# The delta rule's triangular inverse: the level of 16 made by a second substitution on VectorE, the first one moved a turn earlier, and the lanes reordered

## The chip, the core and the metric

The kernel runs on one core of a Trainium2 chip. The core has five engines that run at the same time, each through its own queue of instructions in order: TensorE (matrix products; PE in the profile, its weight loads PEld), VectorE (DVE), ScalarE (ACT), GpSimd (POOL) and SyncE (SP), which here issues every DMA. The metric is device time in microseconds (us): the median of a few runs. The profile is one further execution, and has a time of its own.

## The reference

A network of two layers works on 1024 tokens of width 256. Each layer is half an FFN, attention, and half an FFN. The first layer's attention is a windowed softmax attention; the second layer's is a gated delta rule, and only that one is touched here. It has 16 heads with keys and values of 128 channels:

```python
def step(S, inp):
    qt, kt, vt, gt, bt = inp
    S = S * gt[..., None]
    pred = jnp.einsum('bhk,bhkv->bhv', kt, S)
    delta = (vt - pred) * bt[..., None]
    S = S + kt[..., None] * delta[:, :, None, :]
    o = jnp.einsum('bhk,bhkv->bhv', qt, S)
    return (S, o)
```

The kernel does not walk through 1024 steps. It takes chunks of 128 tokens. In a chunk the steps are a triangular system: with M the gated products of the chunk's keys below the diagonal and beta the step sizes, the kernel needs Z, the inverse of a triangular 128x128 matrix, once for each chunk and head. All arithmetic is float32.

## The kernel before

The first 600 us are the first layer and an FFN, the last 60 an FFN; the delta rule (`delta_rule`, from L509) lies between. Its 16 heads are four groups of four (HG); a group has eight chunks, taken two at a time. So there are 16 **pairs** (one group, two chunks: eight triangular matrices), and the work of a pair is made of generators that yield after each step:

- `prepare` (L664): convolves keys and queries (`convolved`, L633: two products on TensorE, one scaling on ScalarE, three multiply-adds on VectorE for each head), norms, gates. It stores `cfd`, the 1024 numbers of beta, to DRAM for `solve` (L687).
- `triangle` (L773): for the levels 1, 2, 4, ..., 64 it multiplies keys with gated keys and queries (`pm`, L791), and gates them further on VectorE (L813) and GpSimd (L819). A level n gives the blocks of M that join two neighbours of size n. Levels below 16 are gathered in the tile `ml` (L854), level 16 in `mt16` (L856), 32 in `mt32`, 64 in `mt64`. After the loop's level 32 it stores `ml` to DRAM as `dm` (L843).
- `solve` (L879): loads the 16x16 diagonal blocks of `dm` back, one block to a partition (`xb`, 64 partitions, L888), and `cfd` as `diag`; inverts all 64 blocks by substitution on VectorE (L899 to L937); stores the inverted blocks and their transposes to DRAM as the block diagonals of two zeroed matrices (L949), and loads those as `z` and `zt` (L951, L954).
- `invert` (L957): doubles the inverted blocks, from 16 to 32, from 32 to 64 and from 64 to 128, on TensorE: `pmz` = M Z (L968), a negating copy `mz` on ScalarE (L976), `dz` (L983, L991), and a copy into `z` and `zt`. For level 16 that copy is three predicated copies on VectorE (L1008, L1010).
- `values` (L745), `gates` (L756): the values' convolution and the output gate.
- `advance` and `emit` (L1038, L1081): the recurrence from chunk to chunk with `zt`, and the output of a chunk.

In turn i (L1130) the lanes work on different pairs: `prepare` on pair i+2, `triangle` on i+1, `solve`, `invert`, `values`, `gates` on i, `advance` and `emit` on i-1. `weave` (L1111) emits their steps by a list written by hand: a lane has a begin, an end (as fractions of the turn) and a count of steps, and its steps are spread evenly between. That sets the order of the program. It is not yet the order on the engines: the kernel is built with `schedule_with_timeline_sim=True` (L1257), where a planner may move an instruction ahead of others on its engine when its own estimate of times says that it is ready.

Most tiles that the change touches have one buffer (the pool `blk`, bufs=1), `ml`, `mt32` and the two DRAM matrices have two, taken in turn (`turns`, L600).

Of the kernel before, what the change touches and what calls it, by code (L numbers as in the profile page):

```python
# [10 lines left out]
F32 = mybir.dt.float32  # L11
# [497 lines left out]
def delta_rule(tc, a, x, xnT, pp, bc, kon, ones, kdw, first):  # L509
# [33 lines left out]
    with ExitStack() as ctx:  # L543
# [57 lines left out]
        for i in range(2):  # L601
            turn = {}
            for nm in ("ml", "mt16", "mt32"):
                turn[nm] = cst.tile([P, 2, HG, 64], F32, name=f"{nm}_{i}")
                nc.gpsimd.memset(turn[nm], 0.0)
            for nm in ("z", "zt"):
                turn[nm] = dram.tile([2, HG, P, P], F32, name=f"{nm}_{i}", bufs=1)
                for c in range(2):
                    for r in range(2):
                        nc.sync.dma_start(  # L610
                            out=turn[nm][c].rearrange("h r s -> r h s")[:, :, 64 * r : 64 * r + 64],
                            in_=turn["mt16"][:, c],
                        )
# [159 lines left out]
        def triangle(us):  # L773
# [11 lines left out]
            for i, n in enumerate(LEVELS):  # L785
# [43 lines left out]
                if n == 32:  # L829
# [8 lines left out]
                    for c, u in enumerate(us):  # L838

                        dm = u["dm"] = dram.tile([HG, P + 1, 64], F32, name="dm", bufs=4)  # L840
                        for half in (lo, hi):
                            r0 = half.start + half.start // 64
                            nc.sync.dma_start(  # L843
                                out=dm[:, r0 : r0 + 64, :].rearrange("h r s -> r h s"), in_=turn["ml"][half, c]
# [8 lines left out]
                if n < BLK:  # L853
                    nc.vector.copy_predicated(dst(flat(turn["ml"])), pred4, run4(pm[:, 0]))  # L854
                else:
                    nc.vector.tensor_mul(dst(flat(turn["mt16"])), run4(pm[:, 0]), run4(all_heads(mask)))  # L856
# [15 lines left out]
        def blocks(ap):  # L872
# [3 lines left out]
                tensor=ap.tensor, offset=ap.offset, ap=[[BLK * (pitch + 1), P // BLK], [pitch, BLK], [1, BLK]]  # L876
            )

        def solve(us, vb):  # L879
# [5 lines left out]
            for c, u in enumerate(us):  # L885
                for h in range(HG):
                    q0 = 32 * c + 8 * h
                    nc.sync.dma_start(  # L888
                        out=xb[q0 : q0 + 8].rearrange("b (i j) -> b i j", j=BLK),
                        in_=blocks(u["dm"][h]),  # L890
                    )
# [49 lines left out]
            )  # L941
            z = us[0]["z2"] = lev.tile([P, 2, HG, 64], F32, name="z", bufs=1)
            zt = us[0]["zt2"] = lev.tile([P, 2, HG, P], F32, name="zt", bufs=2)
            for c, u in enumerate(us):
                for got, to in ((zb, "z"), (ztb, "zt")):
                    full = u["p"]["turn"][to][c]
                    for h in range(HG):
                        q0 = 32 * c + 8 * h
# [312 lines left out]
```

## Time and profile before

| | |
|---|---|
| median of 3 runs | 1785.18 us (1783.14 to 1787.38) |
| the profiled execution | 1795.66 us, of which the span of the core's instructions 1793.8 us |
| delta rule, about | 605 to 1730 us |
| mean granted TensorE clock | 0.897 |
| DMA, q1, share of 16 engines | 12.8% |

The profile's page and the trace give instructions in groups: line of the kernel, engine, operation, the tiles written and read (out<-in), their shapes and count, then the busy time in us and the mean of one in ns, and after the second bar how long the engine stood idle before them and what ended that. A view of waits says who waited for whom, in total us, times and the longest. "SPq" is a DMA being issued on SyncE's queue; if its duration is long, SyncE waited inside that row. The duration in such a row is not the transfer. The page's chain of waits goes back from the last instruction to what released it; its largest shares by line are 5% for the products of the convolutions (L641) and 4% for DMA `dm<-ml`.

### The profile page before, as it was taken

The page shows a single profiled execution, that of the slowest core. Times are in us where ns is not written, and L with a number is a line of the kernel's source. Part 1 is how long each engine was busy: PE and PEld are TensorE (multiplying, and loading weights), DVE is VectorE, ACT ScalarE, POOL GpSimd, SP SyncE. Part 2 cuts the span into 40 slices and gives each one's busy share as a digit, 9 for nine tenths or more (in the row PEclk, how much of TensorE's full clock was granted, in tenths as well). Part 3 has the DMA queues.
Part 4 walks back from the last instruction along what each step waited for, and adds up shares of the span by engine and source line. Part 5 has one row for each costly group of instructions (what it writes and reads, how often), then busy time and mean ns, then how long its engine had stood idle before and what let it go on. Part 6 is the DMA issues. An engine that isn't in the chain of part 4 may idle for free.

```text
span 1793.8 us, 33380 instructions
## 1 busy us (share of the span) xinstructions
PE 1532.6 (85%) x13152; PEld 1107.1 (62%) x13152; DVE 1186.9 (66%) x2569; ACT 831.3 (46%) x1981; POOL 526.4 (29%) x470
## 2 busy tenths in 40 slices
PE   7886868777999766789989889898999898998879
PEld 3434445545555555667767677677778776776745
DVE  3999977584232357667678678876768877877221
ACT  2117273746122344536645645654665564563320
POOL 0022223231001034335434434433434442543100
PEclk9997989889999766789889989989889988989989
DMA  7020000002002001021111121102120120111100
GB/s 241 32 54 26 3 19 1 1 1 66 0 0 47 1 7 23 10 52 28 24 15 43 21 56 22 30 12 44 38 50 15 22 47 9 40 24 23 56 0 24
DMA packets 150348, 54.94 MB, mean 31 GB/s; under 512 B 116784, under 2 KB 142704, under 8 KB 149936
## 3 DMA queue, kind: packets, MB, share of 16 engines
q1 hardware_dynamic: 150192, 52.81, 12.8%
q8 instruction: 104, 1.70, 0.4%
q14 instruction: 52, 0.43, 0.1%
HBM read 39.11 MB, written 11.70 MB: 28 GB/s over the span
## 4 chain that ended last, share of the span: by engine, by line
PE 41%; DVE 26%; ACT 11%; DMA 9%; issue 6%; POOL 4%; SPq 3%; another core or an unknown queue 1%; DVEq 0%; POOLq 0%; ACTq 0%
PE ps L641 5%; DMA dm<-ml 4%; PE po L160 4%; PE pg L135 3%; PE pu L135 3%; DVE kq L813 3%; ACT e L319 3%; PE pm L791 2%; PE pr L253 2%; DVE k L655 2%; PE pg L700 2%; PE px L1101 2%; DVE other L195 2%; PE po L365 2%; DVE other L208 2%
## 5 line engine op out<-in xcount | busy, mean ns | idle before, releaser
L819 POOL TENSOR_TENSOR k<-k,d 128x512 f32<-128x512 f32 x96 | 149.7, 1559 | 312.2 <-PE pm L791 190.6
L791 PE MATMUL pm<-kq,k 128*64 128x64 f32 x3072 | 133.5, 235 | 29.9 <-POOL kq L742 11.5
L791 PEld LDWEIGHTS pm<-kq,k 128*64 128x64 f32 x3072 | 113.3, 146 | 62.0 <-issue 40.0
L813 DVE TENSOR_TENSOR kq<-kq,d 128x1024 f32<-128x1024 f32 x96 | 130.8, 1363 | 17.8 <-PE pm L791 6.7
L319 ACT ACTIVATE e<-ps,nm 128x128 f32<-128x128 f32 x256 | 91.5, 397 | 63.6 <-DVE nm L314 62.3
L655 DVE SCALAR_TENSOR_TENSOR k<-ps,pp,k 128x256 f32<-128x256 f32 x192 | 84.7, 473 | 27.0 <-ACT k L653 25.5
L655 DVE SCALAR_TENSOR_TENSOR q<-ps,pp,q 128x256 f32<-128x256 f32 x192 | 86.2, 478 | 22.7 <-ACT q L653 20.0
L655 DVE SCALAR_TENSOR_TENSOR v<-ps,pp,v 128x256 f32<-128x256 f32 x192 | 87.5, 474 | 19.8 <-ACT v L653 18.5
L253 PE MATMUL pr<-xnT,wq 128*128 128x512 f32 x128 | 64.7, 641 | 22.1 <-DVE nm L314 10.6
L641 PE MATMUL ps<-xnT,wv 128*128 128x259 f32 x256 | 79.5, 439 | 2.7 <-DVE v L655 1.5
L983 PE MATMUL dz<-mz,zt 64*64 64x32 f32 x768 | 74.9, 230 | 8.0 <-ACT mz L976 8.0
L991 PE MATMUL dz<-zt,mz 64*64 64x32 f32 x1024 | 81.4, 234 | 0.0
L641 PE MATMUL ps<-xnT,wq 128*128 128x259 f32 x256 | 78.6, 442 | 0.4 <-DVE ss L681 0.2
L365 PE MATMUL po<-wo,oT 128*128 128x256 f32 x256 | 64.1, 394 | 13.7 <-ACT oT L362 12.4
L991 PEld LDWEIGHTS dz<-zt,mz 64*64 64x64 f32 x1024 | 67.3, 147 | 12.4 <-issue 10.6
L1101 PE MATMUL px<-wdo,oT 128*128 128x256 f32 x256 | 70.4, 421 | 5.1 <-ACT oT L1097 5.1
L641 PE MATMUL ps<-xnT,wk 128*128 128x259 f32 x256 | 71.8, 418 | 1.0 <-ACT k L653 0.5
L742 POOL TENSOR_TENSOR kq<-q,ge 128x1024 f32<-128x1024 f32 x16 | 51.3, 3209 | 70.3 <-PE pso L1073 40.0
L653 ACT ACTIVATE q<-ps,pp 128x256 f32<-128x256 f32 x64 | 30.4, 474 | 89.1 <-PE ps L641 86.5
L968 PE MATMUL pmz<-z,mt 64*64 64x64 f32 x1024 | 56.1, 233 | 18.0 <-DMA z<-z 13.7
L968 PEld LDWEIGHTS pmz<-z,mt 64*64 64x64 f32 x1024 | 42.9, 140 | 44.4 <-issue 17.8
L708 ACT ACTIVATE gy<-pg,pp 128x256 f32<-128x256 f32 x64 | 29.4, 474 | 85.4 <-PE pg L700 67.5
(215 smaller groups left out, 3953.5 us busy)
## 6 DMA issues: line engine op xcount, KB each, us to landing
zt<-zt SPq DMA_DIRECT2D x32, 256.0 KB
dm<-ml SPq DMA_DIRECT2D x64, 64.0 KB
z<-z SPq DMA_DIRECT2D x64, 64.0 KB
wq<-in_aWq SPq DMA_DIRECT2D x1, 2048.0 KB
wo<-in_aWo SPq DMA_DIRECT2D x1, 2048.0 KB
wk<-in_dWk SPq DMA_DIRECT2D x4, 512.0 KB
wq<-in_dWq SPq DMA_DIRECT2D x4, 512.0 KB
wv<-in_dWv SPq DMA_DIRECT2D x4, 512.0 KB
```

Of the source, the lines that this page charges most:

```text
L135: nc.tensor.matmul(ps[:n], lhsT=w[:, c, cs], rhs=xnT[:, c, cols], start=(c == 0), stop=(c == KC - 1))
L253: nc.tensor.matmul(pr, lhsT=w[:, c, hcol : hcol + HD], rhs=xnT[:, c, PAD + hf * 512 : PAD + (hf + 1) * 512], start=(c == 0), stop=(c == KC ...
L319: nc.scalar.activation(e[:, s, j, :], ps[:, s, j, :], AF.Exp, bias=nm[:, 4 * s + j : 4 * s + j + 1], scale=SUB**-0.5, accum_out=z[:, s, j ...
L365: nc.tensor.matmul(po, lhsT=oT[:, h, :], rhs=wpool["wo"][:, g * HG + h, :], start=(h == 0), stop=(h == HG - 1),)
L641: nc.tensor.matmul(ps[:, 0 : 2 * P + 3], lhsT=w[nm][:, c, h * HD : (h + 1) * HD], rhs=xnT[:, c, PAD + t0 - 3 : PAD + t0 + 2 * P], start=(c ...
L655: nc.vector.scalar_tensor_tensor(yh, xi, pp[:, col : col + 1], yh, ALU.mult, ALU.add)
L791: nc.tensor.matmul(pm[half, :, c * HG + h, :].rearrange("p b (s l) -> p b s l", l=n), lhsT=k[:, c, h, half], rhs=rights(kq[:, :, c, h, half]),
L813: nc.vector.tensor_mul(kqr, kqr, dl.unsqueeze(1).unsqueeze(3).to_broadcast([P, 2, 2 * HG * runs, n]),)
L819: nc.gpsimd.tensor_mul(kl, kl, dr.unsqueeze(2).to_broadcast([P, 2 * HG * runs, n]))
L968: nc.tensor.matmul(pmz[half, c, h], lhsT=p["turn"][f"mt{n}"][half, c, h], rhs=z[half, c, h], start=True, stop=True,)
L991: nc.tensor.matmul(runs(dz[half, 1, c, h]), lhsT=mz[half, c, h], rhs=right(zt[half, c, h, half], n), start=True, stop=True,)
L1101: nc.tensor.matmul(px, lhsT=oT[:, h, :], rhs=u["w"]["o"][:, h, :], start=(h == 0), stop=(h == HG - 1))
```

## The change

Level 16 is no longer made by `invert` on TensorE. `triangle` puts the products of level 16 into `ml` with the smaller ones, and `dm` then holds, beside the 16x16 blocks of the diagonal, the 16x16 blocks that join two of them. `solve` loads these too, four times over, into 128 partitions (`mb`: partition 32 j + b holds joint b, for the columns 4 j to 4 j + 3), and copies its own inverted blocks between partitions (`z1`, `z2`). A new generator, `join`, makes - Z22 M21 Z11 on VectorE by two broadcast products and two reductions, and stores the result to DRAM beside the block diagonals; then it loads `z` and `zt`, which `solve` did before. `invert` begins at 32. `solve` works on pair i+1 in the turn of its `triangle`, and not on pair i. Stores and loads of single heads are merged (`xb` one instruction, the block diagonals two). The fractions of the lanes are changed.

```diff
-                if n < BLK:
-                    nc.vector.copy_predicated(dst(flat(turn["ml"])), pred4, run4(pm[:, 0]))
-                else:
-                    nc.vector.tensor_mul(dst(flat(turn["mt16"])), run4(pm[:, 0]), run4(all_heads(mask)))
+                nc.vector.copy_predicated(dst(flat(turn["ml"])), pred4, run4(pm[:, 0]))
...
-            for c, u in enumerate(us):
-                for h in range(HG):
-                    q0 = 32 * c + 8 * h
-                    nc.sync.dma_start(
-                        out=xb[q0 : q0 + 8].rearrange("b (i j) -> b i j", j=BLK),
-                        in_=blocks(u["dm"][h]),
-                    )
+            dm = us[0]["dm"]
+            nc.sync.dma_start(
+                out=xb.rearrange("b (i j) -> b i j", j=BLK),
+                in_=blocks(dm, (BLK, BLK, 64), (1, 0, BLK), (0, 1, BLK)),
+            )
+            mb = blk.tile([P, BLK, BLK], F32, name="mb")
+            for j in range(4):
+                nc.sync.dma_start(
+                    out=mb[32 * j : 32 * j + 32],
+                    in_=blocks(dm, (32, 32, 32), (1, 0, BLK), (0, 1, BLK), col=BLK),
+                )
...
+            z1 = blk.tile([P, 4, BLK], F32, name="z1")
+            z2 = blk.tile([P, BLK, BLK], F32, name="z22")
+            for j in range(4):
+                at = slice(32 * j, 32 * j + 32)
+                nc.sync.dma_start(out=z1[at], in_=ztb[0:64:2, 4 * j : 4 * j + 4, :])
+                nc.sync.dma_start(out=z2[at], in_=zb[1:64:2])
+            rows = ((BLK, BLK, 64), (1, 0, BLK), (0, 1, BLK))
+            for got, to in ((zb, "z"), (ztb, "zt")):
+                nc.sync.dma_start(out=blocks(us[0]["p"]["turn"][to], *rows), in_=got)
+            us[0]["blocks"] = mb, z1, z2
+            yield
+
+        def join(us):
+            mb, z1, z2 = us[0]["blocks"]
+            turn = us[0]["p"]["turn"]
+            four = blk.tile([P, 4, BLK, BLK], F32, name="four")
+            nc.vector.tensor_mul(
+                four,
+                mb.rearrange("p r s -> p s r").unsqueeze(1).to_broadcast([P, 4, BLK, BLK]),
+                z1.unsqueeze(2).to_broadcast([P, 4, BLK, BLK]),
+            )
+            yield
+            mz1 = blk.tile([P, 4, BLK], F32, name="mz1")
+            nc.vector.tensor_reduce(mz1, four, AX.X, ALU.add)
+            yield
+            nc.vector.tensor_mul(
+                four,
+                z2.unsqueeze(1).to_broadcast([P, 4, BLK, BLK]),
+                mz1.unsqueeze(2).to_broadcast([P, 4, BLK, BLK]),
+            )
+            yield
+            add = blk.tile([P, 4, BLK], F32, name="add")
+            nc.vector.tensor_reduce(add, four, AX.X, ALU.add)
+            z21 = blk.tile([P, BLK, 4], F32, name="z21")
+            nc.scalar.mul(z21, add.rearrange("p j i -> p i j"), -1.0)
+            zt21 = blk.tile([P, 4, BLK], F32, name="zt21")
+            nc.scalar.mul(zt21, add, -1.0)
+            yield
+            for j in range(4):
+                at = slice(32 * j, 32 * j + 32)
+                nc.sync.dma_start(
+                    out=blocks(turn["zt"], (32, 32, 32), (1, 0, 4), (0, 1, BLK), row=4 * j, col=BLK), in_=zt21[at]
+                )
+                nc.sync.dma_start(
+                    out=blocks(turn["z"], (32, 32, 32), (1, 0, BLK), (0, 1, 4), row=BLK, col=4 * j), in_=z21[at]
+                )
...
+            for c in range(2):
+                of = lambda to: turn[to][c * HG : (c + 1) * HG, 0:P]
+                nc.sync.dma_start(out=zt[:, c], in_=of("zt").rearrange("h r s -> r h s"))
+                for r in (lo, hi):
+                    nc.sync.dma_start(out=z[r, c], in_=of("z")[:, r, r].rearrange("h r s -> r h s"))
             yield
...
-            for n in (16, 32):
...
-                    nc.vector.copy_predicated(side(z, 0), pred(slice(0, P), K_T), runs4(dz[:, 0]))
-                    for half in (lo, hi):
-                        nc.vector.copy_predicated(
-                            side(zt[half, :, :, half], 1), pred(half, K_M + i * 32), runs4(dz[half, 1])
-                        )
...
             if past:
-                lanes.append((0.5, 0.8, 12, chain(advance(past[0]), emit(past[0]), advance(past[1]), emit(past[1]))))
+                lanes.append((0.0, 0.4, 12, chain(advance(past[0]), emit(past[0]), advance(past[1]), emit(past[1]))))
             if now:
-                lanes.append((0.1, 0.2, 14, solve(now, vbs[i % 2])))
-                lanes.append((0.3, 0.95, 8, invert(now)))
-                lanes.append((0.55, 0.7, 7, values(now)))
+                lanes.append((0.0, 0.2, 5, join(now)))
+                lanes.append((0.75, 0.9, 5, invert(now)))
+                lanes.append((0.05, 0.7, 7, values(now)))
             if mid:
-                lanes.append((0.2, 0.85, 9, triangle(mid)))
+                lanes.append((0.1, 0.6, 9, triangle(mid)))
+                lanes.append((0.55, 0.9, 14, solve(mid, vbs[i % 2])))
             if ahead:
-                lanes.append((0.0, 0.3, 21, prepare(ahead)))
+                lanes.append((0.1, 1.0, 21, prepare(ahead)))
```

## The prediction

> **What bounds the kernel now.** I read the page for the engines' shares, then the sums of the stretch in which the delta rule runs evenly, then the waits of that stretch, then SyncE's order around the longest of them.
>
> The page, part 1 (engine, busy us, share of the span, instructions):
>
> ```profile
> PE 1532.6 (85%) x13152; PEld 1107.1 (62%) x13152; DVE 1186.9 (66%) x2569; ACT 831.3 (46%) x1981; POOL 526.4 (29%) x470
> ```
>
> The stretch from 760 to 1605 us: thirteen pairs in 845 us, so 65 us a pair.
>
> ```profile
> core 0: us, PE busy (x) PEld busy (x) DVE busy (x) ACT busy (x) POOL busy (x), PEclk, DMA share, GB/s
> 760.00:1605.00 845.00, 769.01 (x8986) 619.21 (x8985) 633.14 (x1257) 475.00 (x821) 349.00 (x305) 0.91 0.16 31
> ```
>
> Per pair TensorE is busy 59.2 us, VectorE 48.7. Both are close to the 65, and neither is the only bound: in the whole page's chain PE has 41%, DVE 26%, ACT 11%, DMA 9%. VectorE's waits in the same stretch (who waits for whom: us in total, times, longest us):
>
> ```profile
> DVE nb L899 <- DMA xb<-dm: 74.6, 13, 10.5
> DVE k L655 <- ACT k L653: 18.9, 16, 2.7
> DVE v L655 <- ACT v L653: 18.3, 18, 2.6
> DVE s L1067 <- PE pn L1059: 16.7, 8, 5.0
> DVE kq L741 <- PE pso L1073: 15.4, 10, 3.0
> ```
>
> The largest is 74.6 / 13 = 5.7 us a pair, at the first instruction of `solve`. All the other lines of that view sum to 127.0, or 9.8 a pair. So the ledger of VectorE is 48.7 busy + 5.7 + 9.8 + 0.8 unnamed = 65. SyncE's queue in two pairs says what the 5.7 is (start, us, line, what, count):
>
> ```profile
> 983.40 1.26 SPq L843 DMA_DIRECT2D dm<-ml  x2
> 984.75 0.56 SPq L687 DMA_DIRECT2D cfd<-cf  x1
> 985.35 1.29 SPq L843 DMA_DIRECT2D dm<-ml  x2
> 986.74 12.02 SPq L888 DMA_DIRECT2D xb<-dm  x8
> ...
> 1368.47 0.39 SPq L687 DMA_DIRECT2D cfd<-cf  x1
> 1376.20 3.45 SPq L843 DMA_DIRECT2D dm<-ml  x4
> 1380.54 2.85 SPq L888 DMA_DIRECT2D xb<-dm  x8
> ```
>
> Eight loads take 2.85 us to issue where `cfd` was stored 8 us earlier, and 12.02 where `cfd` was stored between the `dm`. L687 writes 4 KB as 1024 single floats. What is queued behind that store lands about 12 us after it; VectorE stands still at L899 (10.21 us idle there in this pair). Note also that these loads, which the program puts half a turn after the store, come directly behind it: the planner moves instructions, so places in a turn are wishes and not times.
>
> **The change, part by part**, per pair, 16 pairs.
>
> *Removed, TensorE.* 32 products `pmz` and 64 `dz` (each product is two instructions): 16 `pmz` start within 959.92 to 960.53 us, 38 ns each; 24 `dz` within 974.71 to 975.53, 34 ns each. 32 x 38 + 64 x 34 = 3.4 us. (The groups' busy sums would say 7.4, but their rows overlap.) TensorE falls from 59.2 to 55.8.
>
> *Removed, VectorE and ScalarE.* One predicated copy of 436 ns (L1008), two of 427 (L1010): 1.3 us. ScalarE loses one `mz` of 595 ns and gets two `mul` of 128x64. The nearest ScalarE row (128x128, L339) is 342 ns, so at most 0.7 us: even. At level 16 a multiplication of 413 ns becomes a predicated copy of some 570: +0.16.
>
> *Added, VectorE: `join`.* Groups that show the kinds (line, engine, operation, tiles, shapes, count | busy us, mean ns | idle before):
>
> ```profile
> L313 DVE TENSOR_REDUCE nm<-ps 128x8 f32<-128x1024 f32 x32 | 38.5, 1210 | 0.4 <-PE ps L302 0.3
> ...
> L741 DVE TENSOR_TENSOR kq<-k,ge 128x1024 f32<-128x1024 f32 x16 | 21.5, 1344 | 15.5 <-PE pso L1073 15.4 <-ACT ge L722 0.2
> ...
> L920 DVE TENSOR_TENSOR tmp<-nb,vb 64x512 f32<-64x512 f32 x16 | 18.4, 1148 | 0.4
> ```
>
> Two reductions of 1024: 2 x 1.21 = 2.4. The second product reads along the row: 1.34 as L741. The first reads `mb` down a column, 64 bytes from element to element. L920 reads so, at 2.24 ns an element against 1.31 in L741. The Trainium skill (SBUF — State Buffer, "Door 1: The DMA port swizzle") says that an access that crosses to another 16-byte line pays a penalty, which fits L920. By the plain row the product would be 1.34, by L920 doubled 2.30; I take 2.3. Join: 2.4 + 1.3 + 2.3 = 6.0 us. VectorE's net is 6.0 + 0.2 - 1.3 = +4.9, to 53.6. That half of the lanes were idle before (64 partitions) saves nothing here; the level is new work for this engine.
>
> *DMAs.* SyncE issues 35 per pair before (4 `dm`, diag, 8 `xb`, 16 blocks, 2 + 4 loads) and 34 after (4, diag, 1 `xb`, 4 `mb`, 8 `z1`/`z2`, 2 blocks, 8 of `zt21`/`z21`, 2 + 4). At some 0.35 to 0.63 each the queue's time is the same. The `z`/`zt` zero fill at the start moves the same bytes.
>
> *Moved: `solve` into the turn of `triangle`, its loads at 0.56 of a turn, `dm` at 0.41.* That would be 10 us apart; `cfd` stands at 0.72, behind both (before: 0.21, ahead of `dm` at 0.6). `dm` now waits for level 16 as well, one level later. If places hold, `dm` lands in the 2 us of a quiet pair and the wait of 5.7 falls to some 0.5. If the planner puts `cfd` next to `dm` again, it stays 5.7.
>
> *New waits.* `join` waits for `z1`/`z2`, eight small loads behind `solve`; on VectorE whatever is queued behind `four` waits too (the products of `triangle`, the convolutions). Nearest row: the eight `xb` loads, 2.85 us to issue and some 2 to land. From 0 (placed well behind, 0.9 of a turn against 0.0 of the next) to 5; I take 2, nearer to a planned distance than to none. `z21` is stored as 2048 pieces of 16 bytes, and the loads of `z`/`zt` wait for them on SyncE, with `dm` and `xb` of the next pair queued behind. Two rows bracket it: the 64-byte blocks (`z<-zb`, in the chain 1.9 to 3.6 us), and `cfd` with 4-byte pieces, 12 us for 1024. The Trainium skill (DMA: Bandwidth & Descriptors, "Specifications") speaks against this change: below 512 B a transfer is said to be read-modify-write. But 64-byte and 256-byte pieces land in 2 to 4 us here, so the trace puts the cliff lower than the rule does. By the 64-byte row `z21` costs about 4 us, under the 0.55 turns (36 us) that `invert` is set behind, so nothing; by `cfd`'s 12 ns a piece it would be 24 us. I take the first for the likeliest time and keep the second as a rival. The two ends on SyncE are 0 and about 5 us a pair.
>
> *Moved: `advance` to the front, `invert` late, `prepare` spread over the turn.* `prepare`'s convolutions are filler; spread, they stand behind the chain and not ahead of it. All of the other waits (9.8) are VectorE arriving before TensorE or ScalarE. With 4.9 us more work on VectorE and 3.4 less on TensorE a part of them is filled; from 0 to 6, I take 3, below the 5.8 of ACT `k`, `v` and PE `pn`, `pso` together, since order can also add some.
>
> *Fill and drain.* In the last pair `zt` is ready at 1684.9 and first read at 1698.9 (L1052): 14 us of slack cover the longer chain. Without cover it costs up to 10 us once. I take 0.
>
> **Sum**, VectorE's ledger: 53.6 + 0.5 + 2 + (9.8 - 3) + 0.8 = 63.7, or -1.3 us a pair, above TensorE's 55.8. 16 x -1.3 = -21 us on the profiled execution's 1795.66 (span 1793.8). That one lies 0.6% above the median; the difference is carried over: 1785 - 21 = 1764.
>
> **Rivals.**
> A, forecast, 1740 to 1781: as above; what is late next is VectorE itself. Chance 0.40.
> B, much faster: the filling is whole (-6), join waits 0: 53.6 + 0.5 + 3.8 + 0.8 = 58.7, still above TensorE's 55.8; with half a wait more, about 61, -4 x 16 = -64: 1720. For it: TensorE has 9 us idle per pair then. Against: at 88% busy VectorE would have to run nearly without waits. Chance 0.13.
> C, slower: `z21`'s 16-byte pieces land like `cfd`'s, 24 us; SyncE stands at the loads of `z` and the next pair's `dm` and `xb` sit behind them. L899's 5.2 us come back: 63.7 + 5.2 = 68.9, +3.9 x 16 = +62: 1847. It decides from the point where the landing is longer than the gap from `z21`'s place (0.18) to `dm` (0.41), 15 us. For it: twice `cfd`'s pieces. Against: four pieces to a run of 64 bytes against its sixteen. Chance 0.25.
> D, slower by VectorE alone: no wait is filled: 66.7, +1.7 x 16 = +27: 1812. Chance 0.13.
> E, no change: the planner puts `xb` behind `dm` and `cfd` as before, the level's exchange cancels: 1785. Chance 0.09.
>
> **Numbers.** A measurement can tell 0.2% (3.6 us) from no change. Faster: A's 0.40 and B's 0.13, 0.53; same: E, 0.09; slower: C and D, 0.38. The range leaves out the lower half of B and the upper part of C, about 0.18: 1717 to 1842. A's own range is 1740 to 1781.
>
> **What would show it.** The wait of `nb` for `xb` below 20 us in all, and `cfd` more than 10 us away from `dm` in SyncE's order: the moved `solve`. A wait of `four` for `z1` above 50 us: the new wait is mis-sized. The loads of `z` waiting over 10 us behind `z21` on SyncE: C. Rows of `join` summing to 6.0 us and 1536 fewer matrix instructions confirm the costs. I am wrong if VectorE's busy time rises by 4.9 a pair and its other waits don't shrink.

## The result: 3.7% slower

| | before | after |
|---|---|---|
| median | 1784.44 us (1783.14 to 1787.38) | 1851.8 us (1844.79 to 1855.34) |
| ratio to before, 95% interval | | 1.0368 [1.0344, 1.0393] |
| span of the profiled execution | 1793.8 us | 1848.1 us |
| mean granted TensorE clock in it | 0.897 | 0.873 |

The forecast was 1764 us, faster, with a range to 1842. The time is 5.0% above the forecast and 0.5% above the end of the range.

The profile after, page part 1. The two sizes that the change was about are there: 13152 matrix instructions have become 11616 (1536 fewer), and VectorE's busy time has risen.

```profile
PE 1487.0 (80%) x11616; PEld 1079.7 (58%) x11616; DVE 1244.4 (67%) x2585; ACT 823.0 (45%) x1997; POOL 536.0 (29%) x468
```

The steady stretch after, thirteen pairs again. It is now 880 us long, 67.7 a pair: TensorE 55.8, VectorE 51.9.

```profile
core 0: us, PE busy (x) PEld busy (x) DVE busy (x) ACT busy (x) POOL busy (x), PEclk, DMA share, GB/s
780.00:1660.00 880.00, 725.31 (x7577) 591.66 (x7578) 674.47 (x1249) 462.19 (x821) 354.73 (x297) 0.87 0.20 34
```

The rows of `join` after (groups, as in the prediction). 1904 + 1704 + 1210 + 1201 ns are 6.0 us a pair, the predicted size; the product that reads down the columns (L971) is the longer one. The first waits for its operands for 5.9 us in all 16 pairs, so this new wait is next to nothing.

```profile
L971 DVE TENSOR_TENSOR four<-mb,z 128x1024 f32<-128x1024 f32 x16 | 30.5, 1904 | 5.9 <-DMA z<-ztb 5.1 <-DMA z<-zb 0.8
L980 DVE TENSOR_TENSOR four<-z,mz 128x1024 f32<-128x1024 f32 x16 | 27.3, 1704 | 0.0
L978 DVE TENSOR_REDUCE mz<-four 128x64 f32<-128x1024 f32 x16 | 19.4, 1210 | 0.0
L987 DVE TENSOR_REDUCE add<-four 128x64 f32<-128x1024 f32 x16 | 19.2, 1201 | 0.0
```

VectorE's waits in that stretch, after. The wait of `nb` is down from 74.6 to 36.4 us, and waits on the other engines, which the prediction wanted filled, stand in its place.

```profile
DVE nb L910 <- DMA xb<-dm: 36.4, 13, 8.0
DVE gy L723 <- ACT ge L721: 35.5, 12, 4.2
DVE qk L739 <- PE pq L735: 28.3, 13, 3.8
DVE x L1130 <- PE px L1127: 15.2, 11, 4.3
DVE kq L816 <- PE pm L794: 14.3, 12, 2.1
```

A ledger of one turn puts it together: the mean of twelve turns, from one inverse's `zb` to the next. Busy is time covered by at least one row of the engine (neighbouring rows overlap by some 0.1 us, so four rows of 6.0 cover a little less), and idle is the rest. The last line is a kernel of the experiments, the changed one without `join`'s work.

| us a pair | turn | TensorE busy | VectorE busy | VectorE idle | of it for DMA | for ScalarE | for TensorE |
|---|---|---|---|---|---|---|---|
| before | 64.3 | 58.5 | 48.6 | 15.7 | 5.5 | 4.4 | 3.8 |
| after | 68.6 | 56.4 | 52.7 | 15.9 | 3.1 | 4.4 | 6.9 |
| after, without `join`'s work | 64.9 | 55.3 | 48.4 | 16.5 | 2.5 | 5.0 | 7.3 |

VectorE has 4.1 us more to do and the turn is 4.3 longer. Its idle time is what it was: 2.4 us less for DMAs, 3.1 more for TensorE. The last line says that this exchange came with the moved lanes and not with `join`'s work: without that work the waits for TensorE and ScalarE are larger still.

One pair shows where `join` stands. VectorE after, with one row of ScalarE (start, us, engine, line and tiles; in brackets the idle time before a row and what ended it):

```profile
896.30 1.23 DVE L723 SCALAR_TENSOR_TENSOR gy<-gy,ge 128x1024 f32<-128x1024 f32 x1 [4.19 <-ACT ge L721]
897.44 1.88 DVE L971 TENSOR_TENSOR four<-mb,z 128x1024 f32<-128x1024 f32 x1
898.31 1.70 ACT L725 ACTIVATE ge<-gy,nea 128x256 f32<-128x256 f32 x4
...
900.61 1.22 DVE L978 TENSOR_REDUCE mz<-four 128x64 f32<-128x1024 f32 x1
...
902.13 1.39 DVE L744 TENSOR_TENSOR kq<-k,ge 128x1024 f32<-128x1024 f32 x1
...
904.83 1.68 DVE L980 TENSOR_TENSOR four<-z,mz 128x1024 f32<-128x1024 f32 x1
```

and TensorE at the same time:

```profile
895.83 1.04 PE L644 MATMUL ps<-xnT,wk 128*128 128x259 f32 x4
903.67 1.98 PE L794 MATMUL pm<-kq,k 128*64 128x64 f32 x32 [6.80 <-DVE kq L744]
907.04 2.07 PE L644 MATMUL ps<-xnT,wv 128*128 128x259 f32 x4 [1.40 <-DVE v L658]
```

The first products of `triangle` (L794) need `kq`, and TensorE stands still for 6.80 us until VectorE has made it. Most of that is the chain of the gates: `ge` (L725) is ready at 900.0. But from 896.30 on VectorE works without a gap, among it two of `join`'s rows (3.1 us), and comes to `kq` 2.1 us after `ge` was ready. GpSimd has its half of `kq` at 902.4, so `join` can have cost up to 1.1 us of this gap. VectorE's idle time, 4.19 us here, lies just before: it had no room where `join` ran.

### The profile page after: what moved, and what is told of

It reads as the page before. It is cut to its first block, busy times and chain, and to the rows that moved or that the text cites. A ratio compares the mean times of both kernels' runs of the same rounds, so it can differ in the third digit from the quotient of the medians.

```text
span 1848.1 us, 30386 instructions
## 1 busy us (share of the span) xinstructions
PE 1487.0 (80%) x11616; PEld 1079.7 (58%) x11616; DVE 1244.4 (67%) x2585; ACT 823.0 (45%) x1997; POOL 536.0 (29%) x468
## 4 chain that ended last, share of the span: by engine, by line
PE 40%; DVE 27%; ACT 11%; issue 8%; DMA 7%; POOL 4%; SPq 3%; another core or an unknown queue 0%; DVEq 0%; ACTq 0%; POOLq 0%
PE ps L644 4%; PE po L160 4%; PE pg L135 3%; PE pu L135 3%; PE px L1127 3%; PE pm L794 3%; DVE kq L816 3%; ACT e L319 3%; DMA dm<-ml 2%; DVE k L658 2%; PE pr L253 2%; DMA xb<-dm 2%; DVE other L195 2%; PE po L365 2%; PE pss L681 2%
## 5 line engine op out<-in xcount | busy, mean ns | idle before, releaser
L794 PE MATMUL pm<-kq,k 128*64 128x64 f32 x3072 | 144.1, 255 | 101.6 <-DVE kq L744 44.9
L794 PEld LDWEIGHTS pm<-kq,k 128*64 128x64 f32 x3072 | 127.2, 166 | 131.7 <-issue 93.7
L319 ACT ACTIVATE e<-ps,nm 128x128 f32<-128x128 f32 x256 | 91.2, 394 | 64.4 <-DVE nm L314 63.1
L658 DVE SCALAR_TENSOR_TENSOR v<-ps,pp,v 128x256 f32<-128x256 f32 x192 | 88.4, 476 | 14.0 <-ACT v L656 13.1
L644 PE MATMUL ps<-xnT,wk 128*128 128x259 f32 x256 | 83.9, 465 | 16.3 <-DVE k L658 15.5
L644 PEld LDWEIGHTS ps<-xnT,wk 128*128 128x128 f32 x256 | 56.0, 231 | 29.0 <-ACT zt L991 11.4
L644 PEld LDWEIGHTS ps<-xnT,wv 128*128 128x128 f32 x256 | 56.3, 240 | 27.4 <-issue 6.2
L346 POOL TENSOR_TENSOR d<-d,dz 128x512 f32<-128x512 f32 x32 | 34.5, 1077 | 118.4 <-DVE dz L345 82.7
L1127 PEld LDWEIGHTS px<-wdo,oT 128*128 128x128 f32 x256 | 57.1, 232 | 16.4 <-ACT oT L1123 6.0
L656 ACT ACTIVATE v<-ps,pp 128x256 f32<-128x256 f32 x64 | 29.6, 467 | 82.4 <-PE ps L644 82.3
L365 PEld LDWEIGHTS po<-wo,oT 128*128 128x128 f32 x256 | 47.9, 194 | 29.1 <-ACT oT L362 17.2
L950 POOL TENSOR_TENSOR ztb<-vb,diag 64x256 f32<-64x256 f32 x16 | 14.4, 902 | 172.5 <-DVE vb L945 142.8
```

Source lines behind the costliest of these rows:

```text
L319: nc.scalar.activation(e[:, s, j, :], ps[:, s, j, :], AF.Exp, bias=nm[:, 4 * s + j : 4 * s + j + 1], scale=SUB**-0.5, accum_out=z[:, s, j ...
L365: nc.tensor.matmul(po, lhsT=oT[:, h, :], rhs=wpool["wo"][:, g * HG + h, :], start=(h == 0), stop=(h == HG - 1),)
L644: nc.tensor.matmul(ps[:, 0 : 2 * P + 3], lhsT=w[nm][:, c, h * HD : (h + 1) * HD], rhs=xnT[:, c, PAD + t0 - 3 : PAD + t0 + 2 * P], start=(c ...
L658: nc.vector.scalar_tensor_tensor(yh, xi, pp[:, col : col + 1], yh, ALU.mult, ALU.add)
L794: nc.tensor.matmul(pm[half, :, c * HG + h, :].rearrange("p b (s l) -> p b s l", l=n), lhsT=k[:, c, h, half], rhs=rights(kq[:, :, c, h, half]),
L1127: nc.tensor.matmul(px, lhsT=oT[:, h, :], rhs=u["w"]["o"][:, h, :], start=(h == 0), stop=(h == HG - 1))
```

## The experiments

Each ratio is to the kernel before, on the same chip. The expectations carry letters of their own, which are not the cases A to E of the prediction. O says that the new order of lanes costs the time; V that the time of a pair grows with the work that stands in VectorE's order, whatever it is for; D that `join`'s trips through DRAM, its 16-byte stores and the chain behind them cost it (the prediction's C is one form of that); L that the longer path from the substitution over `join` to `z` does. In the last four kernels P says that any edit disturbs the planned order and that this costs, and C that the place of the added work decides.

### Order or arithmetic (four kernels)

**The changed arithmetic in the lanes of before** (level 16 on VectorE, `solve`, `join` and the rest at the old fractions):

```diff
-                lanes.append((0.0, 0.2, 5, join(now)))
-                lanes.append((0.75, 0.9, 5, invert(now)))
+                lanes.append((0.1, 0.2, 14, solve(now, vbs[i % 2])))
+                lanes.append((0.2, 0.3, 5, join(now)))
+                lanes.append((0.3, 0.95, 5, invert(now)))
...
-                lanes.append((0.55, 0.9, 14, solve(mid, vbs[i % 2])))
...
-                lanes.append((0.1, 1.0, 21, prepare(ahead)))
+                lanes.append((0.0, 0.3, 21, prepare(ahead)))
```

> The changed arithmetic (level 16 in join on VectorE) with the order of before: solve, join and invert on pair i in turn i, prepare at 0 to 0.3, triangle 0.2 to 0.85, advance 0.5 to 0.8. Theory O (the new order costs the time: prepare, spread to the end of the turn, sets the gates' chain of Exp and Ln directly ahead of triangle): the loss goes away, 0.985 to 1.00 of before, and the wait of the first pm for kq L744 falls from 45 us to below 15. Theory V (join's 5.6 us of work on VectorE cost it, wherever they stand): 1.025 to 1.04. Theory D (join's extra trips through DRAM, and its stores in pieces of 16 bytes, cost it): 1.025 to 1.04 as well, with waits for z and z1 above 60 us on PE or DVE.

1921.69 us, 1.0796 [1.0753, 1.0838].

**The arithmetic of before in the new lanes** (on the kernel before; `invert` keeps its level 16 on TensorE; the lines that these replace are left out):

```diff
+                lanes.append((0.0, 0.4, 12, chain(advance(past[0]), emit(past[0]), advance(past[1]), emit(past[1]))))
+                lanes.append((0.65, 0.85, 8, invert(now)))
+                lanes.append((0.05, 0.7, 7, values(now)))
+                lanes.append((0.1, 0.6, 9, triangle(mid)))
+                lanes.append((0.55, 0.9, 14, solve(mid, vbs[i % 2])))
+                lanes.append((0.1, 1.0, 21, prepare(ahead)))
```

> The arithmetic of before with the order of the change: solve on pair i+1 at 0.55 to 0.9, invert at 0.65 to 0.85, prepare spread over 0.1 to 1.0, advance 0 to 0.4. Theory O: slower, 1.03 to 1.045. Theories V and D: 0.98 to 1.00, since neither join nor its stores are there.

1779.42 us, 0.9998 [0.9972, 1.0024].

**The changed kernel with `prepare` back at the front of the turn:**

```diff
-                lanes.append((0.1, 1.0, 21, prepare(ahead)))
+                lanes.append((0.0, 0.3, 21, prepare(ahead)))
```

> The changed kernel with one number pair changed back: prepare at 0 to 0.3 of the turn as before. Theory O, if prepare is what matters in it: 0.995 to 1.01. V and D: 1.03 to 1.04.

1899.08 us, 1.0668 [1.0625, 1.0712].

**The kernel before with `prepare` spread** (the same line, the other way round):

> The kernel before with one number pair changed: prepare spread over 0.1 to 1.0 of the turn. Theory O with prepare as its cause: 1.02 to 1.04. V and D: 0.995 to 1.005.

1777.43 us, 0.9996 [0.9971, 1.0021].

O falls. The new order by itself changes nothing, and with the new arithmetic it saves half of what would be lost: 8.0% in the old lanes, 6.7% with only `prepare` as before, 3.7% as changed. The arithmetic costs the time. The 8.0 and 6.7% lie above what any of the theories had expected. So which part of it costs, its work on VectorE, its transfers or its longer path?

### Work or transfers (four kernels)

**The changed kernel without `join`'s work.** The two products and two reductions over 1024 elements become two products of 64 elements; loads, stores and copies stay. Level 16 of the inverse is thus not computed.

```diff
-            nc.vector.tensor_reduce(mz1, four, AX.X, ALU.add)
+            nc.vector.tensor_mul(mz1, mb[:, 0:4], z1)
...
-            nc.vector.tensor_reduce(add, four, AX.X, ALU.add)
+            nc.vector.tensor_mul(add, z2[:, 0:4], mz1)
...
-                lanes.append((0.0, 0.2, 5, join(now)))
+                lanes.append((0.0, 0.2, 3, join(now)))
```

> The changed kernel with join's two broadcast products and two reductions of 1024 replaced by two products of 64 elements, so that level 16 of the inverse is not computed; all loads, stores, waits and the order are as in the change. 5.6 us of VectorE per pair are gone. Theory V (VectorE's added work passes into the turn one to one): 0.98 to 1.00 of before. Theory D (the trips through DRAM and the longer chain cost it): 1.025 to 1.04, as the change.

1771.81 us, 0.9899 [0.9857, 0.9942]. The whole loss is gone, as V expected and D did not, with a gain of 1.0% under it. The 2048 pieces of 16 bytes are all still stored in this kernel, so they cost nothing like the 62 us of the prediction's C. Nor are the loads behind them held up after the change. SyncE's waits in the steady stretch: the loads of `zt` behind the stores of `zt21` (64-byte pieces), and in the last line the loads of `z` behind the stores of `z21` (16-byte pieces):

```profile
SPq L998 <- ACT zt L991: 166.3, 11, 17.0
...
SPq L1005 <- DMA zt<-zt: 12.6, 13, 2.2
...
SPq L1007 <- DMA z<-z: 0.9, 2, 0.5
```

2.2 and 0.5 us at most. The long line waits for `join`'s result, not for a transfer.

**The changed kernel without the stores of `z21` and `zt21`** (the eight DMAs of `join` left out, so the blocks of level 16 are missing from the inverse):

> The changed kernel without the stores of zt21 and z21, so that level 16's blocks are missing from z and zt; join's work on VectorE stays, but the loads of z and zt need not wait for it. Theory D: 0.99 to 1.01. Theory V: 1.025 to 1.04. If the 16-byte pieces alone were at fault (rival C of the prediction), this run gives the whole loss back.

1800.21 us, 1.0085 [1.0062, 1.0108]. 2.8% better than the changed kernel, where D had expected it, and well below what V had. All of `join`'s work is still there, and most of the loss is not. It is no proof that the transfers cost that: nothing then waits for `join`'s result, so its four instructions are freer in their place. VectorE's busy time is 53.5 us a pair and its idle time fell to 13.1, against 48.4 and 16.5 without the work: here the work did fill waits. So in the changed kernel the work costs its full time only together with what waits for its result; the path and its stores add up to 2.8%.

**The changed kernel with `join`'s work twice** (each of the four instructions issued twice):

> The changed kernel with each of join's four VectorE instructions made twice in a row: 5.6 us of VectorE more per pair, nothing else. Theory V: 1.08 to 1.09 (another 16 x 5.6 = 90 us). Theory D: 1.04 to 1.055.

1967.49 us, 1.1013 [1.0972, 1.1054], above both expectations. The excess over the added work goes along with a longer wait of VectorE at `nb`: 97.8 us for `xb` over the whole run against 40.4 in the changed kernel. SyncE's queue in one pair shows how: it stands from 1139 to 1172 us, until the stores of `join`'s result (L1014) can go, and the next pair's `cfd`, `dm` and `xb` come behind, with `cfd` directly ahead of `dm` again.

```profile
1138.55 0.49 SPq L888 DMA_DIRECT2D diag<-cfd  x1
1172.39 0.33 SPq L1014 DMA_DIRECT2D z<-z  x1
...
1182.73 0.60 SPq L690 DMA_DIRECT2D cfd<-cf  x1
1183.38 6.27 SPq L847 DMA_DIRECT2D dm<-ml  x4
1195.11 0.59 SPq L891 DMA_DIRECT2D xb<-dm  x1
```

**The kernel before with that work as ballast.** Two products of 1024 and two reductions, of which nobody reads the result, behind the substitution:

```diff
+        def ballast(us):
+            zb, ztb = us[0]["zb"]
+            four = blk.tile([64, 4, BLK, BLK], F32, name="four")
+            nc.vector.tensor_mul(
+                four,
+                zb.rearrange("p r s -> p s r").unsqueeze(1).to_broadcast([64, 4, BLK, BLK]),
+                zb[:, 0:4].unsqueeze(2).to_broadcast([64, 4, BLK, BLK]),
+            )
+            yield
+            mz1 = blk.tile([64, 4, BLK], F32, name="mz1")
+            nc.vector.tensor_reduce(mz1, four, AX.X, ALU.add)
...
+                lanes.append((0.2, 0.4, 4, ballast(now)))
```

> The kernel before with join's four VectorE instructions added as ballast behind solve (same element counts and patterns on 64 partitions, result unused), no DMA and no wait of another engine for them. Theory V: 1.03 to 1.05. Theory D: 1.00 to 1.015, since VectorE stands idle a quarter of the time before.

1880.24 us, 1.0528 [1.0485, 1.0571]. No new DMA, no new path, no result that anything waits for, and a loss is there, larger than the change's: a little more than V expected, far more than D. The same lanes with the whole change cost 8.0%, so there the path or the transfers add to it. The page of this kernel, part 1:

```profile
span 1875.5 us, 33553 instructions
...
PE 1537.1 (82%) x13152; PEld 1118.2 (60%) x13152; DVE 1282.7 (68%) x2633; ACT 829.6 (44%) x1981; POOL 536.9 (29%) x470
```

VectorE has 95.8 us more than before (1186.9), the span 81.7 (1793.8).

How the changed kernel loses it is seen in the idle time of TensorE before `triangle`'s products, the figure after the second bar: before, after, without `join`'s work, and without its stores.

```profile
L791 PE MATMUL pm<-kq,k 128*64 128x64 f32 x3072 | 133.5, 235 | 29.9 <-POOL kq L742 11.5 <-DVE kq L813 10.7 <-issue 5.8
```

```profile
L794 PE MATMUL pm<-kq,k 128*64 128x64 f32 x3072 | 144.1, 255 | 101.6 <-DVE kq L744 44.9 <-POOL kq L745 18.1 <-DVE kq L816 15.3
```

```profile
L794 PE MATMUL pm<-kq,k 128*64 128x64 f32 x3072 | 136.1, 245 | 64.9 <-POOL kq L745 22.6 <-DVE kq L816 15.2 <-DVE kq L744 11.7
```

```profile
L794 PE MATMUL pm<-kq,k 128*64 128x64 f32 x3072 | 139.4, 249 | 65.6 <-DVE kq L744 22.8 <-POOL kq L745 15.5 <-POOL k L822 10.7
```

In the new lanes `triangle` waits for `kq` in any case, 64.9 us against 29.9. `join`'s work adds 36.7 to it, nearly all at the `kq` of VectorE (44.9 against 11.7), and adds nothing to the sum where its result is not stored (65.6). With the ballast this wait grows by 15.5 us only (to 45.4); there the delay passes through other waits.

### Is it VectorE alone? (four kernels)

**The changed kernel with `join`'s two products on GpSimd** (`nc.vector.tensor_mul` becomes `nc.gpsimd.tensor_mul` twice):

> The changed kernel with join's two broadcast products made on GpSimd, its two reductions left on VectorE; all DMAs, waits and the order as in the change, and join's chain is longer (GpSimd needed 3.2 us for 1024 elements before). Theory V (work on VectorE passes into the turn one to one): 3.6 us of VectorE less per pair, 58 us in all: 1.00 to 1.015 of before. Theory L (what costs is that z waits for the whole of join, so the length of the chain decides): 1.035 to 1.05.

1833.97 us, 1.027 [1.0221, 1.0319], between what V and L expected. The products take 2830 and 2416 ns there. VectorE's busy time falls by 28.7 us only, though the products had taken 57.8 there (its other rows became longer), GpSimd gains 83.9, and the span falls by 12.6: it doesn't tell the two apart.

**The kernel before with as much ballast on ScalarE**, the least loaded engine but GpSimd (46% of the span), five dead copies of 1.04 us in the same lane:

```diff
+            for _ in range(5):
+                nc.scalar.copy(four, zb.unsqueeze(1).to_broadcast([64, 4, BLK, BLK]))
+                yield
...
+                lanes.append((0.2, 0.4, 5, ballast(now)))
```

> The kernel before with 5.3 us of ballast per pair on ScalarE in the place where run f4 had it on VectorE (five copies of 64x1024, result unused). Theory V (VectorE is the engine whose work decides): 1.00 to 1.015. If any engine's work added at that place lengthens the turn as in f4: 1.04 to 1.06.

1879.36 us, 1.0547 [1.0515, 1.0578]: as much as on VectorE. So V falls as far as it says that VectorE alone decides. VectorE's idle time rises here from 15.7 to 21.4 us a pair while its work stays at 48.5. ScalarE's order in one pair of this kernel:

```profile
1029.72 0.58 ACT L770 ACTIVATE sg<-pgo 128x512 f32<-128x512 f32 x1
1030.20 1.04 ACT L962 COPY four<-zb 64x1024 f32<-64x1024 f32 x1
1031.13 0.47 ACT L653 ACTIVATE k<-ps,pp 128x256 f32<-128x256 f32 x1
1031.50 1.04 ACT L962 COPY four<-zb 64x1024 f32<-64x1024 f32 x1
1032.43 0.48 ACT L653 ACTIVATE k<-ps,pp 128x256 f32<-128x256 f32 x1
```

The copies alternate with the scalings of the next pair's keys, each of which VectorE and then TensorE wait for. An engine that is busy less than half of the time had no room there.

**The kernel before with less work on VectorE** (the sums of squares of the output's norm taken along by ScalarE, 32 reductions fewer, and `prepare` spread):

```diff
-            nc.scalar.square(sq, o)
-            nc.vector.tensor_reduce(m, sq, AX.X, ALU.add)
+            for h in range(HG):
+                nc.scalar.activation(sq[:, h], o[:, h], AF.Square, accum_out=m[:, h : h + 1])
```

> The kernel before with prepare spread over 0.1 to 1.0 (1.00 by itself, run e4), and in emit the squares summed by ScalarE's accumulator, four heads one by one, instead of one square on ScalarE and one reduction on VectorE: 1.36 us of VectorE less per pair, some 3 us of ScalarE more. Theory V: 16 x 1.36 = 22 us, 0.985 to 0.992. If VectorE's work counts only where it is added to a chain: 0.998 to 1.005.

1796.7 us, 1.0089 [1.0051, 1.0127]. It says little: VectorE's busy time did not fall against the spread kernel (1181.6 us against 1177.5), though 32 instructions were gone, and ScalarE's rose by 20.0. The opposite of the ballast isn't shown.

**The kernel before with `cfd` stored in rows.** This tests the other reading of the prediction, that 4-byte pieces hold up `dm` and `xb`. The store now has runs of 32 bytes; eight loads gather the numbers instead of one.

```diff
-            cfd = us[0]["cfd"] = dram.tile([2, HG, P], F32, name="cfd", bufs=4)
-            nc.sync.dma_start(out=cfd.rearrange("c h r -> r c h"), in_=cf)
+            cfd = us[0]["cfd"] = dram.tile([P, 2, HG], F32, name="cfd", bufs=4)
+            nc.sync.dma_start(out=cfd, in_=cf)
...
-            nc.sync.dma_start(out=diag, in_=us[0]["cfd"].rearrange("c h (b i) -> (c h b) i", i=BLK))
+            for q in range(2 * HG):
+                nc.sync.dma_start(
+                    out=diag[8 * q : 8 * q + 8],
+                    in_=cfd[:, q // HG, q % HG].rearrange("(b i) -> b i", i=BLK),
+                )
```

> The kernel before with cfd stored in rows of 32 bytes instead of 1024 single floats, and diag gathered by eight loads instead of one. The first part of the prediction (cfd's 4-byte pieces hold up the dm stores behind them): the wait of nb for xb falls from 84.7 us to below 30. If a shorter wait shortens the turn: 0.955 to 0.985. If VectorE's idle time is of a fixed size and only moves (theory V): 0.99 to 1.005.

1733.14 us, 0.9723 [0.9697, 0.9749], the fastest kernel of this study. SyncE's queue in a pair where the store stands between the `dm`, as in the one shown before:

```profile
953.96 1.28 SPq L843 DMA_DIRECT2D dm<-ml  x2
955.34 0.54 SPq L687 DMA_DIRECT2D cfd<-cf  x1
955.93 1.24 SPq L843 DMA_DIRECT2D dm<-ml  x2
957.27 3.01 SPq L893 DMA_DIRECT2D xb<-dm  x8
```

The loads take 3.01 us to issue and not 12.02. VectorE's wait of `nb` over the whole run falls from 84.7 to 32.9 us, 51.8; the time falls by 52.6. The equality is partly chance: a turn is 4.7 us shorter (59.6), 3.9 of it from VectorE's waits for DMAs.

### How much, where, and do the two add? (four kernels)

**The ballast made tiny** (four instructions of 16 elements in the same places):

> Run f4 with ballast of 16 elements in place of 1024: four VectorE instructions at the same place, some 0.6 us together in place of 5.6. Theory P (any edit disturbs the planned order, and that costs): 1.03 to 1.06. Theory V or C (work, or work on the chain): 1.00 to 1.01.

1800.12 us, 1.0089 [1.0054, 1.0123]. Four more instructions, and the other order that the planner then finds, come with 0.9%, so P falls for the most part. The rest of the ballast's 5.3% came with its duration; its order under the longer rows is not the same one, so the split is not exact.

**The ballast late in the turn** (0.85 to 1.0 in place of 0.2 to 0.4):

> Run f4 with its 5.6 us of ballast per pair at 0.85 to 1.0 of the turn in place of 0.2 to 0.4, behind solve and nearly all of invert. Theory V (the amount decides): 1.04 to 1.06, as f4. Theory C (the place decides: ahead of the next pair's convolutions and products it lies on the chain that passes through all engines): 1.00 to 1.025.

1876.25 us, 1.052 [1.0473, 1.0567], the same as early, for a plain reason: the planner put the ballast back. One pair, early and late:

```profile
1159.08 0.41 DVE L937 TENSOR_TENSOR zb<-vb,diag 64x256 f32<-64x256 f32 x1
1159.52 1.91 DVE L961 TENSOR_TENSOR four<-zb 64x1024 f32<-64x1024 f32 x1
```

```profile
1150.88 0.41 DVE L937 TENSOR_TENSOR zb<-vb,diag 64x256 f32<-64x256 f32 x1
1151.32 1.91 DVE L961 TENSOR_TENSOR four<-zb 64x1024 f32<-64x1024 f32 x1
```

In both traces all 2633 rows of VectorE stand in the same order, and so do those of ScalarE, GpSimd and SyncE. So this is a second run of the ballast kernel. It repeats the loss, and leaves C, that the place decides, untested.

**The changed kernel with `cfd` in rows:**

> The changed kernel with cfd stored in rows of 32 bytes. If the two losses are separate and add: 1.037 - 0.028, 1.005 to 1.015. If the new order already keeps cfd away from dm: 1.03 to 1.04.

1789.13 us, 1.0016 [1.0000, 1.0033]. Against the changed kernel's 1.0368 that is 3.4% less, a little more than the 2.8% from the kernel before. So the two losses are separate: the cost of `join` stays, and `cfd`'s wait goes from either kernel.

**The kernel before with `prepare` spread and `cfd` in rows:**

> The kernel before with prepare spread (run e4, 1.00) and cfd in rows: if the gain of cfd in rows (run h2, 0.972) adds to the order's: 0.965 to 0.975. If the spread order already had the gain of the shorter wait for xb and lost it elsewhere: 0.99 to 1.00.

1782.54 us, 0.9979 [0.9954, 1.0003]. No gain beyond the spread kernel's 0.9996. There the wait of `nb` was small already (12.8 us against 84.7), so there was little left to remove. The spread order had removed the same stall and gained nothing by it: VectorE waited for TensorE and ScalarE (8.0 and 5.4 us a pair) in its place. Shorter `nb` waits are worth 2.8% only where no other wait takes their place.

### The sum over all of them

Work added on one engine and the time that came with it, both from the same two profiled executions:

| from, to | engine | busy, us | span, us |
|---|---|---|---|
| before, tiny ballast | VectorE | +10.0 | +6.5 |
| before, ballast early | VectorE | +95.8 | +81.7 |
| before, ballast late | VectorE | +94.8 | +76.6 |
| before, ballast | ScalarE | +75.1 | +81.5 |
| changed without `join`'s work, changed | VectorE | +67.0 | +76.2 |
| changed, `join`'s work twice | VectorE | +79.5 | +122.0 |
| changed without `join`'s work, changed without its stores | VectorE | +76.2 | +26.6 |

In six of the seven most of it is paid. In the last, where the result is not stored, two thirds are hidden. And VectorE's idle time per pair, from the ledger as above:

| | turn | VectorE busy | VectorE idle |
|---|---|---|---|
| before | 64.3 | 48.6 | 15.7 |
| before, ballast early | 69.8 | 54.3 | 15.5 |
| before, ballast late | 69.9 | 54.2 | 15.7 |
| changed, without `join`'s work | 64.9 | 48.4 | 16.5 |
| changed | 68.6 | 52.7 | 15.9 |
| changed, without `join`'s stores | 66.5 | 53.5 | 13.1 |
| changed, `join`'s work twice | 77.6 | 57.6 | 20.0 |
| changed arithmetic, lanes of before | 74.0 | 53.2 | 20.8 |
| before, `prepare` spread | 63.7 | 48.0 | 15.7 |
| before, `cfd` in rows | 59.6 | 48.7 | 10.9 |
| changed, `cfd` in rows | 64.4 | 53.2 | 11.3 |

Work that others wait behind did not shrink the idle time, and two kernels, `join` twice and the changed arithmetic in the old lanes, have more of it. The kernel without the stores is the one where work shrank it. The removal of the `cfd` stall shrinks it by 5 us in two kernels, and moving that stall away by another order (`prepare` spread) doesn't.

## Why the prediction was wrong

**What held.** The cost of `join` (6.0 us a pair), the 1536 instructions fewer on TensorE, the near-zero cost on SyncE, and the reading of `cfd`: it was confirmed by a store in rows, worth 2.8%. That `join` came to 6.0 is partly luck: the plain product took 1.70 us and not 1.34, the one down the column 1.90 and not 2.3, and the two errors cancel. The changed kernel without `join`'s work shows that all the rest of the change, the products taken from TensorE, the merged DMAs and the moves, is worth 1.0% together, about as much as four tiny instructions moved the time (0.9%).

**The step that failed** is in the paragraph on the moved lanes: "With 4.9 us more work on VectorE and 3.4 less on TensorE a part of them is filled; from 0 to 6, I take 3". The waits of VectorE for TensorE and ScalarE did not fall by 3 us a pair; they rose from 8.2 to 11.4. The runs show this in two parts. The first has nothing to do with the added work: without it these waits are 12.3, so what the moved lanes took from the waits for DMAs (5.5 to 2.5) came back as waits for TensorE and ScalarE, and the turn stayed where it was (64.9 against 64.3). The second is the work: 4.4 us of it, and the idle time fell only from 16.5 to 15.9. The prediction took an idle engine for an engine with room. The engines pass work to each other in order: when VectorE stood idle it was waiting for others, and when `join` ran, TensorE was waiting for VectorE (`kq`, 44.9 us against 11.7). Even the value that the prediction named as its bound, 0, was too good. That the work must cost this much by itself is not shown: without its stores the same work cost 1.9% and not 4.7%.

**Terms that were mis-sized.** VectorE's busy time rose by 4.1 and not 4.9 a pair. The new wait of `join` is 0.4 and not 2. The wait of `nb` fell to 2.8 and not to 0.5: `cfd` does stand 6.6 us ahead of `dm` in one pair (1201.31 and 1207.91 us), but the waits are not gone, and the stores in rows recover 3.4% even after the change. In the ledger of the prediction: 48.7 + 4.1 busy, 2.8 and 0.4, and with the turn at 68.6 the remainder, 12.6, is the other waits and what is unnamed; it was 9.8 + 0.8, and forecast as 6.8 + 0.8. Two smaller slips stand in the working. The four waits called 5.8 us together sum to 69.3 us, 5.3 a pair. And the 9.8 are not all for TensorE and ScalarE: 1.2 of them are for GpSimd and for releasers that the profile doesn't name.

**The rivals.** C gave 1847 us, close to the measured 1851.8, and for a wrong reason: the same 16-byte stores stand in the kernel at 0.990. D came nearest in mechanism, VectorE's work with no wait filled, and its 1812 was 40 us too low, since the wait of `nb` fell by half as much as it assumed and the other waits grew. Its test was written down: VectorE's busy time up and its other waits not smaller.

**What stays open.** How the loss divides between `join`'s work and the path behind it. Dead work alone cost 5.3% in the old lanes, and the whole change 8.0% there; in the new lanes the work cost 4.7% with its result stored and 1.9% without. How much of that difference belongs to the path and how much to the planner's freedom to place the work isn't known. Nor is it known whether the dead work would have hidden at another place, as the planner left it where it was. Also open: why the ballast on ScalarE costs somewhat more than its busy time; why `prepare` spread gains nothing from its shorter wait of `nb`; and whether less work on VectorE would give the time back one to one, as the one attempt didn't lessen its busy time. The 0.9% for a change of four tiny instructions warns against reading single differences of that size.

## What to carry to other kernels

The idle share of an engine is not room for work. In a chain that passes through several engines in order, ask of an added instruction what stands behind it in its queue and who waits for its result, and price it in full until a run shows that it hides. That can be tried before anything is rewritten, by putting dead work of the same duration into the kernel as it is: 6 us a pair of it cost 5.3% here, and would have warned of what the ledger missed. Then look in the trace where that work really stands, since a planner may put it where it was before. A stall with a cause of its own, such as a store in single floats ahead of everything else on a queue, was the better thing to look for here.

## What the runs showed of the hardware

**Small pieces.** With a store of 1024 single floats among the `dm`, the loads behind took 12.02 us to issue; with the same store in runs of 32 bytes they took 3.01. The loads of `z` waited at most 0.5 us for the 2048 pieces of 16 bytes, behind loads of `zt` that had waited at most 2.2 for pieces of 64. So of the sizes in these kernels only single floats were seen to hold up a queue; the stores differ in their number of pieces too, so no threshold follows.

**TensorE's clock after a gap.** The clock granted around the gap of 6.80 us shown above, changed kernel, in stretches (start:end, us, busy times, then PEclk):

```profile
core 0: us, PE busy (x) PEld busy (x) DVE busy (x) ACT busy (x) POOL busy (x), PEclk, DMA share, GB/s
892.00:896.90 4.90, 4.87 (x35) 4.24 (x33) 0.71 (x2) 4.86 (x6) 0.00 (x0) 1.00 0.33 44
896.90:900.30 3.40, 0.00 (x0) 0.00 (x0) 3.40 (x5) 3.37 (x7) 0.21 (x1) 0.80 0.00 0
900.30:903.60 3.30, 0.00 (x0) 0.00 (x0) 3.30 (x6) 1.07 (x3) 3.30 (x2) 0.50 0.00 0
903.60:907.00 3.40, 1.98 (x32) 1.82 (x32) 3.40 (x6) 0.00 (x0) 3.37 (x3) 0.50 0.00 0
907.00:910.00 3.00, 2.96 (x7) 2.41 (x8) 3.00 (x5) 0.00 (x0) 2.95 (x4) 0.50 0.00 0
910.00:913.00 3.00, 2.51 (x35) 1.74 (x34) 3.00 (x7) 1.27 (x4) 2.65 (x5) 0.57 0.22 16
913.00:916.00 3.00, 2.16 (x13) 1.71 (x12) 3.00 (x6) 1.81 (x3) 1.68 (x1) 1.00 0.17 9
```

Four convolution products take 1.04 us ahead of the gap and 2.07 behind it. The Trainium skill (TensorE: Matmul & The Clock Gate, Part 1) has the rule for it: an idle window of some 3.4 us takes the clock to half, and about as long a busy one gives it back. This trace agrees in part. The clock falls to half in the gap, some 2 us after the last product (0.80 over the first 3.40 us) and so sooner than the rule has it, and it is back at 1.00 only from 913 us on, after a stretch in which TensorE was busy in part (1.98 of the first 3.40). By the rule a gap costs at least 1.7 us of clock, half of 3.4, so for one gap a pair an estimate of 16 x 1.7 = 27 us; this gap cost more. TensorE's busy time for the same 11616 instructions is 1461.4 us without `join`'s work and 1487.0 with it, 25.6 more. So the clock's own part of those 76.2 us of span is about a third at most, as far as busy time shows it. It is not the cause: with the ballast on VectorE, TensorE's busy time rose by 4.5 us of 81.7.

**The same product on two engines.** The column-wise product of 1024 elements on 128 partitions took 1904 ns on VectorE and 2830 on GpSimd (means); the row-wise one 1704 and 2416. On VectorE the column-wise one was nearly constant (1874 to 1922 ns), the row-wise one was not (1222 to 2191); why isn't shown.
